# Eleven products of constants and a mark by GpSimd ahead of layer 0's experts

## The chip, the core and the metric

The kernel runs on one core of one Trainium2 chip, in one launch. The metric is the device time of an execution in microseconds. The time before is the median of four runs, 1123.99 us (1120.69 to 1127.42).

## The reference

Two transformer layers on a batch of 8 sequences of 512 tokens with 128 channels, all in float32. Each layer has a recurrent attention (a scan over the 512 steps) and a mixture of experts. The change stands between two parts of layer 0's mixture: the routing, which decides for each token which two of eight experts it goes to and which slot it has there, and the experts themselves. Cut to that:

```python
logits = relu(x @ rw1 + rb1) @ rw2 + rb2
vals, ids = top_k(logits, 2)
probs = softmax(vals)
pos = cumsum(one_hot(ids, 8)) - 1              # the slot in the expert
disp[ids, pos] += x                            # 512 slots for each of 8 experts
h = relu(einsum('enc,ech->enh', disp, ew1) + eb1)
eo = einsum('enh,ehc->enc', h, ew2) + eb2
y = eo[ids, pos] * probs * (pos < 512)         # then summed over the two choices
x = x + y
```

Layer 1 takes the sum `x` as its input.

## The kernel before

The program is a sequence of stages, each with tiles of its own in SBUF and PSUM. Within the two big stages (layer 0's attention with its routing; layer 1) a planner in Python, `Order`, decides the order of the instructions from estimated costs when the program is built. It also puts "fills" (L952) into gaps that it expects on TensorE: products of the identity with a tile of zeros, 128x128 by 128x512, into a PSUM bank that nobody reads. The order is then fixed: every engine works through its own instructions in that order, and waits at semaphores for the others.

**The end of the routing.** `route(b)` handles one sequence of 512 tokens, in four tiles of 128. Its last products on TensorE are the two that count the assignments before each token (L860, L861). VectorE computes from them a slot number for each assignment (L865 to L871), and GpSimd scatters the tokens' rows, 130 numbers each (128 channels, the weight, the place to return to), with eight indirect DMAs of 128 rows (L876) into `row0`, a table in DRAM with 512 slots for each of 8 experts.

**The experts of layer 0** (L1021 on) have an order written out by hand. SyncE issues eight loads (L1023), one for each expert's 512 slots, into tiles `de0[e]`; they wait for the scatters' data. For an expert `e`:

- `prepare0(e)`: four transposes on TensorE (L436, called from L984) into `tr_bank`, and a copy by VectorE into `dT0` (L985).
- `first_half(e)`: four products 128x128 by 128x512 (L990), each into a bank of its own, `mid_banks0[0..3]`, and each followed by ScalarE's relu (L993) into `hT0`.
- `second_half(e)`: four products that add up in `yT_bank` (L997), and ScalarE's bias (L1000).
- `results0(e)`: four transposes back (L1005), VectorE's multiply with the weights (L1006), and four indirect DMAs by GpSimd (L1012), which scatter the results to their tokens in `res0`.

TensorE's order is `prepare0(0)`, then for each expert `first_half(e)`, `results0(e - 1)`, `prepare0(e + 1)`, `second_half(e)`. Expert 0's first instruction on TensorE is so the transpose of its first 128 slots. The experts' weights were loaded earlier, during the scans. In layer 1, `attend(b)` loads the results (`ys`, L1149) and adds them to the tokens on TensorE (L1161).

`ident` (the identity), `zeros` (128x512) and the pool `const` are made at the start of the program and stay. The PSUM pool of the experts takes the banks that the stage before gave back: one for `tr_bank`, four `mid_banks0`, one `yT_bank`, two `y_banks`. A product in float32 stands in the trace as two records, a transpose as one.

Of the kernel before, what the change touches and what calls it, by code (L numbers as in the profile page):

```python
# [9 lines left out]
F32 = mybir.dt.float32  # L10
# [7 lines left out]
P = 128  # L18
# [11 lines left out]
NC0 = H0 // P  # L30
# [159 lines left out]
def two_layers(ctx: ExitStack, tc: tile.TileContext, a: dict, out: bass.AP):  # L190
    nc = tc.nc

    const = ctx.enter_context(tc.tile_pool(name="const", bufs=1))
# [10 lines left out]
    def ring_of(pool, n, shape, name, dtype=F32):  # L204
        return [pool.tile(shape, dtype, tag=f"{name}{i}", bufs=1, name=f"{name}{i}") for i in range(n)]
# [19 lines left out]
    ident = const.tile([P, P], F32, name="ident")  # L225
# [102 lines left out]
    zeros = const.tile([P, S], F32, name="zeros")  # L328
# [650 lines left out]
    mid_banks0 = ring_of(psum, 4, columns, "mid0")  # L979
# [3 lines left out]
    def prepare0(e):  # L983
        transpose_to(tr_bank, de0[e][:, :, 0:C])  # L984
        nc.vector.tensor_copy(dT0[e % 2], tr_bank)  # L985

    def first_half(e):
        for c in range(NC0):
            ps = mid_banks0[c]
            nc.tensor.matmul(  # L990
                ps, lhsT=ew1_all[:, e, c * P : (c + 1) * P], rhs=dT0[e % 2], start=True, stop=True
            )
            nc.scalar.activation(hT0[e % 2][:, c, :], ps, AF.Relu, bias=col(EB1 + e * NC0 + c))  # L993

    def second_half(e):
        for c in range(NC0):
            nc.tensor.matmul(  # L997
                yT_bank, lhsT=ew2_all[:, e, c, :], rhs=hT0[e % 2][:, c, :], start=c == 0, stop=c == NC0 - 1
            )
        nc.scalar.activation(yT0[e % 2], yT_bank, AF.Identity, bias=col(EB2 + e))  # L1000

    def results0(e):
        ps, y = y_banks[e % 2], y0[e % 3]
        for t in range(NT):
            nc.tensor.transpose(chunk(ps, t), chunk(yT0[e % 2], t), ident)  # L1005
        nc.vector.tensor_mul(  # L1006
            y,
            tiled(ps),
            de0[e][:, :, WEIGHT : WEIGHT + 1].to_broadcast(tokens),
        )  # L1010
        for t in range(NT):
            nc.gpsimd.indirect_dma_start(  # L1012
                out=res0_w[e * NT + t],
                out_offset=bass.IndirectOffsetOnAxis(ap=de0[e][:, t, DEST : DEST + 1].bitcast(I32), axis=0),
                in_=y[:, t, :],
                in_offset=None,
                bounds_check=NA0 - 1,
                oob_is_err=False,
            )

    with tc.manual_schedule():  # L1021
        for e in range(E0):
            nc.sync.dma_start(de0[e], row0[e * CAP : (e + 1) * CAP, :].rearrange("(t p) c -> p t c", p=P))  # L1023
        prepare0(0)
        for e in range(E0):
            first_half(e)
            if e > 0:
                results0(e - 1)
            if e + 1 < E0:
                prepare0(e + 1)  # L1030
            second_half(e)
        results0(E0 - 1)
        nc.scalar.preload_act_table_set(EXP)
# [777 lines left out]
```

## Time and profile before

| What | Value |
| --- | --- |
| median of four runs | 1123.99 us (1120.69 to 1127.42) |
| the profiled execution | 1118.28 us |
| its span, first to last instruction | 1116.5 us |
| its mean granted TensorE clock | 0.818 |
| PE busy | 832.2 us (75% of the span) |
| VectorE, ScalarE, GpSimd busy | 625.9, 472.5, 453.1 us |
| fills, L952 | 76 records, 42.9 us busy, mean 694 ns |
| L990 PE | 64 records, 31.6 us busy, mean 641 ns, shortest 592, longest 1219 |
| L1012 GpSimd | 32 scatters, 31.3 us busy, mean 979 ns |

The busy time of an engine is an average over stages that have different limits, so the page's shares don't tell what a few microseconds between two stages are worth. For that the timeline of the stretch is read, and for TensorE also the granted clock: 1.00 is full speed, and 0.50 half of it, at which the same product takes twice as long. A stretch's row gives the clock and how much of it the engine had work. Times are from the span's start; routing ends and the experts start between 360 and 400 us.

### The profile page before, as it was taken

What the parts mean: (1) busy time and instruction counts of PE and PEld (TensorE: products, weight loads), DVE (VectorE), ACT (ScalarE), POOL (GpSimd) and SP (SyncE); (2) the same over time, 40 slices, a digit from 0 to 9 for tenths busy, and PEclk for the clock granted to TensorE, in tenths of its full rate; (3) what the DMA queues carried; (4) which work ended last, traced back from release to release, by engine and by line L of the source; (5) the groups of instructions that cost most, each with busy time, mean ns of one, the idle gap of its engine ahead of it and who ended that gap; (6) DMA issues with size and microseconds to landing.
All of it is one profiled execution on the core that took longest, in us unless ns stands there. A gap on an engine that the chain in (4) does not pass through costs nothing. (4 is left out here: it accounts for less than half of the span.)

```text
span 1116.5 us, 13427 instructions
## 1 busy us (share of the span) xinstructions
PE 832.2 (75%) x3819; PEld 552.8 (50%) x3819; DVE 625.9 (56%) x1592; ACT 472.5 (42%) x1040; POOL 453.1 (41%) x466
## 2 busy tenths in 40 slices
PE   5979898897889399687889598655628677777830
PEld 3545464563546144234656345443318577766730
DVE  5588987698693111266776285452435445554417
ACT  6544655462524044385466554433413233332310
POOL 6200005307445334200053548565553656556550
PEclk9887889779788599898899677777758888899775
DMA  7985666474244300389550175461113222222119
GB/s 180 235 220 130 140 160 189 105 176 100 65 96 145 78 11 15 108 219 221 130 147 20 48 191 159 105 184 39 39 57 102 80 78 82 81 77 81 46 31 358
DMA packets 75531, 131.93 MB, mean 118 GB/s; under 512 B 13044, under 2 KB 54902, under 8 KB 67264
## 3 DMA queue, kind: packets, MB, share of 16 engines
q1 hardware_dynamic: 46400, 91.12, 31.7%
q0 software_dynamic: 14832, 27.84, 8.6%
q10 hardware_dynamic: 14224, 12.11, 3.6%
q8 instruction: 30, 0.49, 0.2%
q14 instruction: 45, 0.37, 0.1%
HBM read 94.79 MB, written 41.14 MB: 122 GB/s over the span
## 5 line engine op out<-in xcount | busy, mean ns | idle before, releaser
L1532 POOL DMA_INDIRECT rows<-rows,si x128 | 152.3, 1190 | 215.6 <-DVE tmp L1502 131.7
L1739 POOL DMA_INDIRECT res<-qy,to x144 | 143.0, 993 | 110.3 <-DVE qw L1701 69.1
L876 POOL DMA_INDIRECT row<-rows,si x64 | 90.0, 1406 | 220.0 <-DVE qT L587 112.2
L1718 ACT ACTIVATE qh<-mid,qw 128x128 f32<-128x128 f32 x288 | 78.7, 383 | 180.3 <-remote 91.6
L1712 PE MATMUL mid<-dT,qw 128*128 128x128 f32 x576 | 88.9, 310 | 42.7 <-issue 35.9
L1712 PEld LDWEIGHTS mid<-dT,qw 128*128 128x128 f32 x576 | 80.6, 219 | 49.9 <-issue 42.0
L1729 PE MATMUL qyp<-qw,qh 128*128 128x128 f32 x576 | 81.6, 302 | 5.9 <-ACT qh L1718 3.9
L671 PE MATMUL acc<-add,center 128*128 128x512 f32 x128 | 75.8, 747 | 10.2 <-DVE add L700 8.4
L1729 PEld LDWEIGHTS qyp<-qw,qh 128*128 128x128 f32 x576 | 78.9, 219 | 5.2 <-ACT qh L1718 4.1
L694 DVE TENSOR_TENSOR_SCAN add<-dec,add 128x2048 f32<-128x2048 f32 x16 | 70.8, 4425 | 0.7
L1737 DVE TENSOR_TENSOR qy<-qyp,de 128x512 f32<-128x512 f32 x36 | 24.8, 688 | 75.1 <-remote 26.4
L1701 DVE COPY qw<-fw 128x258 f32 x144 | 44.0, 306 | 35.3 <-issue 16.8
L179 ACT ACT_TABLE_LOAD x48 | 61.6, 1283 | 5.2 <-issue 3.2
L671 PEld LDWEIGHTS acc<-add,center 128*128 128x128 f32 x128 | 29.9, 244 | 52.8 <-issue 34.0
L1012 POOL DMA_INDIRECT res<-y,de x32 | 31.3, 979 | 46.7 <-DVE dT L985 22.1
L952 PE MATMUL idle_bank<-zeros,ident 128*128 128x512 f32 x76 | 42.9, 694 | 0.8 <-DVE y L1006 0.8
L1702 DVE COPY qw<-fw 128x256 f32 x144 | 42.2, 293 | 2.1 <-issue 1.6
L1317 PE MATMUL acc<-ident,kb 128*128 128x128 f32 x256 | 37.2, 315 | 7.3 <-DVE kb L1307 7.3
L1317 PEld LDWEIGHTS acc<-ident,kb 128*128 128x128 f32 x256 | 36.0, 229 | 11.5 <-DVE kb L1307 11.4
L1696 PE MATMUL qT<-ident,de 128*128 128x128 f32 x144 | 25.5, 289 | 21.8 <-DMA de<-rows 14.1
L789 PE MATMUL bank<-xT,rw 128*128 128x512 f32 x64 | 37.8, 723 | 4.2 <-ACT xT L781 3.8
L662 ACT ACTIVATE dec<-dec 128x2048 f32<-128x2048 f32 x16 | 30.5, 1907 | 21.9 <-DVE dec L682 21.9
(336 smaller groups left out, 1766.6 us busy)
## 6 DMA issues: line engine op xcount, KB each, us to landing
add<-keys SPq DMA_DIRECT2D x16, 1024.0 KB
qb_first<-queries SPq DMA_DIRECT2D x8, 1024.0 KB
qb_second<-queries SPq DMA_DIRECT2D x8, 1024.0 KB
kb<-pairs SPq DMA_DIRECT2D x8, 1024.0 KB
gb_both<-decays SPq DMA_DIRECT2D x8, 1024.0 KB
qb_both<-pairs SPq DMA_DIRECT2D x8, 1024.0 KB
yk<-res SPq DMA_DIRECT2D x8, 1024.0 KB
de<-rows SPq DMA_DIRECT2D x108, 65.0 KB
```

What stands on the lines that cost most here:

```text
L179: self.load(table)
L671: nc.tensor.matmul(acc, lhsT=center, rhs=st[:, j, :], start=g + j == 0, stop=(g + 1) * J + j == D + J - 1)
L694: nc.vector.tensor_tensor_scan(flat, dec.rearrange("p j t -> p (j t)"), flat, 0.0, ALU.mult, ALU.add)
L876: nc.gpsimd.indirect_dma_start(out=row0_w[(b * NT + t) * 2 + k], out_offset=bass.IndirectOffsetOnAxis(ap=m.si[:, t, k : k + 1], axis=0), i ...
L952: nc.tensor.matmul(idle_bank, lhsT=ident, rhs=zeros, start=True, stop=True)
L1317: nc.tensor.matmul(chunk(acc, t), lhsT=chunk(st[:, j, :], t), rhs=ident, start=j + t == 0, stop=j + t == DK + NT - 2)
L1532: nc.gpsimd.indirect_dma_start(out=rows1_w[(b * NT + t) * K1 + k], out_offset=bass.IndirectOffsetOnAxis(ap=m.si[:, t, k : k + 1], axis=0), ...
L1701: nc.vector.tensor_copy(w1_q[:, i, :], fw1[:, bass.ds(at, WE)])
L1712: nc.tensor.matmul(mid[c][:, here], lhsT=w1_q[:, i, c * P : (c + 1) * P], rhs=dT[:, here], start=True, stop=True)
L1718: nc.scalar.activation(hT[:, c, here], mid[c][:, here], AF.Gelu, bias=w1_q[:, i, I1 + c : I1 + c + 1])
L1729: nc.tensor.matmul(ps[:, here], lhsT=hT[:, c, here], rhs=w2_q[:, i, c * C : (c + 1) * C], start=c == 0, stop=c == NC1 - 1,)
L1739: nc.gpsimd.indirect_dma_start(out=res1_w[4 * q + i], out_offset=bass.IndirectOffsetOnAxis(ap=to[:, i : i + 1], axis=0), in_=y[:, i, :], i ...
```

## The change

Ahead of the loads of the slots in the text (and so ahead of expert 0's transposes on TensorE) there are now eight products of the identity with `zeros`, into the bank of `mid_banks0[3]`; then GpSimd sets a new tile `gate0` of one column to zero; a product with `gate0` as its moving operand, into the first column of the same bank, makes TensorE wait for that memset; three more products of the identity with `zeros` follow. On GpSimd the memset stands behind the routing's last scatters. The first real product into `mid_banks0[3]`, expert 0's fourth, starts the bank anew, so nothing of what the eleven write is read.

```diff
+    def warm0(n):
+
+        for _ in range(n):
+            nc.tensor.matmul(mid_banks0[NC0 - 1], lhsT=ident, rhs=zeros, start=True, stop=True)
+
+    gate0 = const.tile([P, 1], F32, name="gate0")
     with tc.manual_schedule():
+        warm0(8)
+        nc.gpsimd.memset(gate0, 0.0)
+        nc.tensor.matmul(mid_banks0[NC0 - 1][:, 0:1], lhsT=ident, rhs=gate0, start=True, stop=True)
+        warm0(3)
         for e in range(E0):
             nc.sync.dma_start(de0[e], row0[e * CAP : (e + 1) * CAP, :].rearrange("(t p) c -> p t c", p=P))
         prepare0(0)
```

## The prediction

> **What bounds the kernel now.** I read the page first (span 1116.5 us), then the order of time on TensorE, GpSimd and SyncE between layer 0's routing and its experts, then the stretches' granted clock. In the timeline of TensorE (start, duration, engine, line, what; in brackets the idle time before it and what ended it):
>
> ```profile
> 363.13 0.63 PE L860 MATMUL bank<-both,before 128*128 128x32 f32 x2 [1.07 <-DVE hot L823]
> 363.82 0.63 PE L861 MATMUL bank<-prior,ones 128*128 128x32 f32 x2
> 382.12 1.09 PE L436 MATMUL tr<-ident,de 128*128 128x128 f32 x4 [17.67 <-DMA de<-row]
> 384.05 6.46 PE L990 MATMUL mid<-dT,ew_all 128*128 128x512 f32 x8 [0.84 <-DVE dT L985]
> 390.34 0.60 PE L436 MATMUL tr<-ident,de 128*128 128x128 f32 x4
> 390.77 3.60 PE L997 MATMUL yTp<-hT,ew_all 128*128 128x512 f32 x8
> 394.21 3.60 PE L990 MATMUL mid<-dT,ew_all 128*128 128x512 f32 x8
> 397.64 0.60 PE L1005 MATMUL yp<-ident,yT 128*128 128x128 f32 x4
> ```
>
> TensorE has nothing for 17.67 us, until expert 0's slots land. Then the same work is slow for expert 0 and fast for expert 1: transposes 1.09 against 0.60, four products (eight records, two to a product) 384.05 to 390.34 = 6.29 against 394.21 to 397.64 = 3.43. The timelines of GpSimd and SyncE show what sets the landing: the last two scatters, then the loads.
>
> ```profile
> 375.39 0.97 POOL L876 DMA_INDIRECT row<-rows,si  x1 [0.30 <-issue]
> 376.67 0.97 POOL L876 DMA_INDIRECT row<-rows,si  x1 [0.30 <-issue]
> 379.12 4.71 SPq L1023 DMA_DIRECT2D de<-row  x8
> ```
>
> Stretches (time, length, busy time and count of PE, PEld, DVE, ACT, POOL; granted clock; DMA share; GB/s) give the reason, expert 0's cold clock:
>
> ```profile
> 358.90:362.32 3.42, 3.16 (x9) 1.58 (x8) 1.51 (x13) 0.00 (x0) 2.78 (x3) 0.50 0.02 2
> 365.73:382.80 17.07, 0.68 (x4) 0.71 (x4) 0.56 (x3) 0.00 (x0) 7.83 (x8) 0.50 0.17 43
> 382.80:386.21 3.41, 2.57 (x5) 1.14 (x5) 0.69 (x1) 0.00 (x0) 0.00 (x0) 0.50 1.14 307
> 386.21:389.62 3.41, 3.41 (x5) 1.34 (x5) 0.00 (x0) 1.43 (x3) 0.00 (x0) 0.50 0.46 111
> 389.62:393.04 3.42, 3.42 (x12) 1.69 (x12) 0.69 (x1) 1.32 (x2) 0.00 (x0) 1.00 0.00 0
> ```
>
> The clock changes only at instants a multiple of 3.41 us apart. A cold stretch busy for 2.57 of 3.41 did not raise it; a full one did, at 389.62. Do products of zeros count as work? Yes: the stretch 519.33 to 522.74 below is cold and four fifths fill products (L952, zeros), and 1.00 follows. How little loses a warm clock? 314.53 to 317.94, with 1.39 busy (41%, the end of a run of fills): the product at 318.62 is cold. A stretch 54% busy (447.65 to 451.06) kept it.
>
> ```profile
> 314.53:317.94 3.41, 1.39 (x5) 0.45 (x3) 3.08 (x21) 0.65 (x2) 2.80 (x3) 1.00 0.99 220
> 318.62 2.06 PE L952 MATMUL idle_bank<-zeros,ident 128*128 128x512 f32 x2
> 519.33:522.74 3.41, 3.41 (x5) 1.25 (x5) 1.13 (x4) 2.83 (x6) 0.00 (x0) 0.50 1.04 235
> 522.74:526.16 3.42, 2.53 (x9) 1.18 (x8) 3.42 (x1) 3.40 (x6) 0.00 (x0) 1.00 0.99 223
> ```
>
> From 390.34 on TensorE has no gap until the last expert, 7.75 us an expert (L997 at 390.77 and 398.52). Its end releases the last results' multiply, their scatters, the loads `ys` and layer 1's first products (at 460.67, after 5.76 us of waiting for `ys`). So what expert 0 gains or loses arrives whole at layer 1.
>
> **The change part by part.** Nothing is removed or moved; 12 products, one memset and one wait (TensorE on GpSimd) are added.
>
> The eight. Cold, records of a fill follow each other by 0.85 us (520.88, 521.73), so a product is 1.71; warm by 0.43, so 0.86. They write a bank of the stage before; if it is that of the counts, they wait for DVE L866, whose read ends at 364.78. Bounds: 364.45 (the end of L861) and 365.1; I take 364.8. The stretch 365.73 to 369.14 is then full, so the clock rises at 369.14: cold until there 4.34 us = 2.54 products, the other 5.46 x 0.86 = 4.70, end 373.84. All this hides in the 17.67 us of idle time; without that cover it would be 9 us.
>
> From 373.84 TensorE waits for the mark. The stretch 372.56 to 375.97 is busy for 1.28 of 3.41 (38%), less than the 41% that lost the clock: I let it fall at 375.97. This is the step that could go either way.
>
> The mark. The last scatter is over at 377.64. A memset of 128x1 on GpSimd lasted 0.10 (at 0.33, the start of the program), and an iota behind a scatter began at once (364.85 after 364.84). So it is done at 377.74 at best; 0.30 more as between scatters; or, as the iota L1527 that followed four scatters of layer 0's results did (start 457.66, 1.99 us idle, ended by a DMA), 1.99 later. I take 378.1 for TensorE's start, between the first two, since a constant's memset has no data to wait for. The one-column product: two records of up to 0.27 (L724, 128x1), 0.5 with its weights. Behind the memset on GpSimd's queue stands nothing until the result scatters at 399.72; SyncE's loads wait for the scatters' data and not for it. On TensorE everything stands behind it: three products, then expert 0.
>
> The three start at 378.6. Cold: two end at 382.02; the stretch 379.38 to 382.80 is full, so the clock rises at 382.80; by then 0.78/1.71 = 46% of the third is done and the rest takes 0.54 x 0.86 = 0.47: end 383.27. The slots had come at 382.12, so the three are **1.15 us in the way**.
>
> Expert 0 then runs warm. To its first product: 1.93 (384.05 - 382.12) less 0.49 (1.09 - 0.60) = 1.44, so 384.71; the products 3.43: 388.14 against 390.34. Expert 1's transposes need its slots then: all eight loads are done by 388 (the DMA share falls to 0 there). Sum: -1.15 late, +0.49 and +2.86 (6.29 - 3.43) of warm clock = **2.2 us gained**, 1114.3 for the span 1116.5 and 1116.1 for its execution's 1118.28.
>
> The instants at which the clock may change need not fall so elsewhere. Moved through 3.41 us: the kernel before reaches 390.34 at the latest some 0.2 later and, with the rise at 387.5 instead of 389.62, 1.06 earlier (half of 2.12). The changed one lies between 387.4 (the three raise the clock early and are out of the way by 382.7) and 388.9 (all three cold, end 383.73). Over both the gain is 0.5 to 2.7, about 1.8 in the middle. With the mark 1.99 late it is 1.4 in this run's position and about nothing on average.
>
> The Trainium skill, TensorE: Matmul & The Clock Gate, Part 1, in its table of the two states, takes the clock back only after a window that is idle. By that rule 372.56 to 375.97, in which the eight end, does not count as idle, and the clock would outlive the mark's wait; the three would end at about 381.2 and the gain be 3.4. The row at 314.53 speaks against it (41% busy and lost), and I go by the row.
>
> **The rivals.** (1) The warmth lasts over the wait. For: 54% busy was enough once. Against: 41% was not. Then the three take 2.57 from 378.6, end 381.2 before the slots, and the whole cold loss goes: 0.49 + 2.86 = 3.35, so 1120.6.
>
> (2) Slower: the three, in TensorE's one order, hold expert 0 back. Place: the end of the third against 382.12. Each microsecond past that costs one, and expert 0's warmth returns at most 3.35; so it decides at a third that ends after 385.5, that is, three cold products from a mark after about 379.8. For: L1527's start 1.99 late would put the mark at 379.83. If the mark comes only with the landing of slots (382.1), the products start at 382.6, end cold at 387.7, and expert 1's transposes come at 387.7 + 1.44 + 3.43 = 392.6: 2.3 lost, 1126.3. Against: the iota at 364.85 started at once.
>
> (3) The change does not do what it says: the products of zeros don't raise the clock, and expert 0 is cold as before behind three cold products that end at 383.73: 1.6 lost, 1125.6. Against: 519.33, and with it 795.81 to 799.22.
>
> **How the numbers follow.** The likeliest is the 2.2 of this run's position; on the median of the runs shown, 1123.99 (0.5% above the profiled execution), about 1122. Chances: forecast 0.60, rival 1 0.15, rival 2 0.13, rival 3 0.12. Forecast's own range: 0.5 to 2.7 gained, 1121.3 to 1123.5, and with the scatter of the four runs (-3.3, +3.4) 1118 to 1127. The range with the rivals: from 1120.6 less the scatter to 1126.3 plus most of it: 1116.5 to 1128.5. Of this kernel a measurement can tell 0.5% (5.6 us) from no change. No case by itself reaches that; what lies beyond comes from scatter and costs unseen: 0.13 of the forecast's 0.60 and 0.06 of rival 1's 0.15 faster; 0.09 of rival 2, 0.04 of rival 3 and 0.02 of the forecast slower. Faster 0.19, slower 0.15, same 0.66.
>
> **What would show it.** Eight products from about 364.8 with a clock of 1.00 within 5 us; an idle stretch to about 378; the mark's product at 378.1; the three ending between 381.2 and 383.8; expert 0's four products in 3.4 us and L436 of expert 1 between 387.4 and 388.9. Wrong if the mark comes after 379.8, if the clock is 0.50 in expert 0's products, if a gap opens before expert 1 (slots not there), or if layer 1's first wait for `ys` grows by what was gained.

## The result and the profile after

The changed kernel took 1120.64 us (median of 44 runs, 1113.15 to 1134.15), the kernel before 1119.52 in the runs beside it (70 runs, 1111.85 to 1127.42). The ratio is 1.001, 95% interval 0.9995 to 1.0024: no difference. Here and below a ratio leaves out runs over 1.5% above the fastest of their kernel (beside the e runs of the table, one of 1097.32 us so takes 19 of the 35 with it), and a difference of means takes every run. The changed kernel's profile has a span of 1118.0 us. TensorE's timeline between routing and experts, in the columns used before:

```profile
361.65 0.64 PE L860 MATMUL bank<-both,before 128*128 128x32 f32 x2 [1.23 <-DVE hot L823]
364.22 8.97 PE L1024 MATMUL mid<-zeros,ident 128*128 128x512 f32 x16 [1.25 <-DVE pos L866]
373.03 0.28 PE L1030 MATMUL mid<-gate,ident 128*128 128x1 f32 x2
373.17 2.82 PE L1024 MATMUL mid<-zeros,ident 128*128 128x512 f32 x6
380.68 1.09 PE L436 MATMUL tr<-ident,de 128*128 128x128 f32 x4 [4.69 <-DMA de<-row]
382.61 6.59 PE L990 MATMUL mid<-dT,ew_all 128*128 128x512 f32 x8 [0.84 <-DVE dT L985]
389.04 0.60 PE L436 MATMUL tr<-ident,de 128*128 128x128 f32 x4
```

The eight products (16 records) end at 373.03, the mark's product follows at once, with no idle time, and so do the three. All eleven are over at 375.99. Then TensorE is idle for 4.69 us, and expert 0 is as slow as before: four products in 382.61 to 389.04 = 6.43 us (6.29 before). GpSimd's and SyncE's timelines show that the mark did not stand where it was meant to:

```profile
20.05 0.12 POOL L1029 MEMSET gate<- 128x1 f32 x1
375.14 0.97 POOL L876 DMA_INDIRECT row<-rows,si  x1 [0.30 <-issue]
377.59 4.94 SPq L1033 DMA_DIRECT2D de<-row  x8
```

The memset ran at 20.05 us, between the loads of the constants, 355 us before the last scatter. In GpSimd's order of the built program it stands behind the load of the constant `fb2` and ahead of the first fill of `row0`; the order of every other instruction is unchanged (so the built program lists it; the profile shows the memset's own place). The statement in the description of the change that it stands behind the routing's scatters is how the text reads, and not what was built. So the hand-written order did not hold the memset behind the instructions of an earlier block: the layer that builds the program put a memset that waits for no data early. The eight waited 1.25 us behind DVE L866, for their PSUM bank; that this alone kept them in place is likely and not shown.

The granted clock by stretches (the fields as before: five engines' busy time, then clock, DMA share, GB/s) gives the rest:

```profile
364.57:367.98 3.41, 3.41 (x5) 1.34 (x5) 0.45 (x2) 0.00 (x0) 1.52 (x2) 0.50 0.01 0
367.98:371.39 3.41, 3.41 (x9) 1.50 (x9) 0.00 (x0) 0.00 (x0) 2.50 (x4) 1.00 0.02 2
371.39:374.81 3.42, 3.42 (x11) 1.67 (x10) 0.00 (x0) 0.00 (x0) 2.81 (x3) 1.00 0.03 3
374.81:378.22 3.41, 1.18 (x3) 0.19 (x1) 0.00 (x0) 0.00 (x0) 1.00 (x2) 1.00 0.02 3
378.22:381.63 3.41, 0.95 (x4) 0.71 (x4) 0.00 (x0) 0.00 (x0) 0.00 (x0) 0.50 0.88 236
```

The zeros raised the clock after one full stretch, as worked out. The stretch in which the eleven end is 35% busy, and it lost the clock 2.5 us before the slots came. The first `ys` product of layer 1 starts 78.81 us after the slots' landing (78.55 before). Nothing was gained, and of the stage nothing lost: three profiles without any products (before, g1_before and g4_tile_only in the table below) lie between 77.93 and 78.99.

### The profile page after: what moved, and what is told of

Its sections match the earlier page's. It is cut to its first block, busy times and chain, and to the rows that moved or that the text cites. A ratio compares the mean times of both kernels' runs of the same rounds, so it can differ in the third digit from the quotient of the medians.

```text
span 1118.0 us, 13476 instructions
## 1 busy us (share of the span) xinstructions
PE 840.6 (75%) x3843; PEld 554.8 (50%) x3843; DVE 626.4 (56%) x1592; ACT 472.6 (42%) x1040; POOL 453.0 (41%) x467
## 4 chain that ended last, share of the span: by engine, by line
PE 37%; issue 19%; DVE 15%; DMA 11%; ACT 6%; another core or an unknown queue 5%; POOL 4%; DVEq 1%; SPq 1%; POOLq 0%; ACTq 0%
PE mid L1722 7%; PE qyp L1739 5%; PE acc L671 2%; DMA gb_both<-decays 2%; DVE x L1782 2%; PE acc L1327 2%; PE bank L789 2%; DMA row<-rows,si 2%; POOL res L1012 2%; DVE add L694 2%; PE bank L623 1%; DMA queries<-qT 1%; PE qT L1706 1%; POOL row L876 1%
## 5 line engine op out<-in xcount | busy, mean ns | idle before, releaser
L952 PE MATMUL idle_bank<-zeros,ident 128*128 128x512 f32 x76 | 40.6, 661 | 0.8 <-DVE y L1006 0.8
```

## The experiments

Four theories are told apart. A: the early memset is the whole reason; products that bridge the wait bring about 3 us. B: a mark in its place holds expert 0 back by as much as the warm clock returns. C: what expert 0 gains does not arrive at the end. D came up after the e runs: the new tile costs time of its own. "Landing" is the start of expert 0's first transpose; "tile" says that the kernel has `gate0`, and "warm" kernels are those whose products reach nearly to the landing.

| Run | What | Landing to expert 1's transposes, us | Landing to layer 1's `ys` product, us | Ratio to before (95%) | Difference of means, all runs, us (95%) |
| --- | --- | --- | --- | --- | --- |
| before | | 8.22 | 78.55 | | |
| after | 8, early mark, 3; tile | 8.36 | 78.81 | 1.001 (0.9995 to 1.0024) | +1.4 ± 1.5 |
| e1_mark | 8, mark, 3; tile | 5.01 | 75.43 | 1.003 (0.9999 to 1.006) | +2.7 ± 2.8 |
| e2_sixteen | 16 | 5.00 | 75.91 | 0.9984 (0.9953 to 1.0016) | -3.4 ± 3.2 |
| e3_eight | 8 | 7.76 | 78.25 | 0.9989 (0.9954 to 1.0023) | +0.2 ± 3.2 |
| e4_bridge | 11, mark, 4; tile | 5.01 | 75.45 | 1.0048 (1.0004 to 1.0091) | +1.0 ± 3.1 |
| g1_before | the kernel before | 8.45 | 78.99 | 1.0018 (0.9989 to 1.0048) | +1.3 ± 2.7 |
| g2_sixteen | as e2 | 5.01 | 75.60 | 0.9995 (0.9965 to 1.0025) | -2.4 ± 2.5 |
| g3_bridge_empty | 11, mark, 4; no tile | 5.00 | 75.42 | 0.9977 (0.9941 to 1.0012) | -2.9 ± 3.0 |
| g4_tile_only | tile and memset | 7.68 | 77.93 | 1.0009 (0.9974 to 1.0043) | +0.5 ± 3.3 |
| h1_bridge | as e4; tile | 5.01 | 75.66 | 0.9978 (0.9953 to 1.0002) | -3.8 ± 2.2 |
| h2_bridge_empty | as g3 | 5.01 | 75.38 | 0.9964 (0.9941 to 0.9987) | -5.1 ± 2.3 |
| h3_mark | as e1; tile | 6.70 | 77.06 | 1.0007 (0.9981 to 1.0033) | +0.4 ± 1.9 |
| h4_mark_empty | 8, mark, 3; no tile | 5.19 | 75.58 | 0.9969 (0.994 to 0.9997) | -4.3 ± 2.7 |

Runs whose names begin alike share a chip and 35 runs of the kernel before (medians 1114.06, 1108.89 and 1123.69 us), 12 runs of each variant; they are compared only among themselves.

### The mark in its place, and the wait bridged

e1_mark queues the memset behind the last scatter:

```diff
-                nc.gpsimd.indirect_dma_start(
+                scattered[0] = nc.gpsimd.indirect_dma_start(
...
         warm0(8)
-        nc.gpsimd.memset(gate0, 0.0)
+        with tc.issue_after(scattered[0].ins):
+            nc.gpsimd.memset(gate0, 0.0)
```

> The changed kernel with the memset queued on GpSimd behind the routing's last scatter, by an edge that only orders the issue. Measure: from the start of L860 (the counts) to expert 1's transposes (the second L436), 27.21 us before (363.13 to 390.34) and 27.39 with the change (361.65 to 389.04). Theory A (the change's memset stood at 20.1 us, so its mark held nothing and the eleven products ended 4.7 us too early): the mark's product now comes 0.1 to 0.5 us after the last scatter, the three end 0.5 us before to 1.6 us after the slots come, the clock is 1.00 before expert 0's first product ends, the stretch is 24.5 to 26.7 us, and 0.5 to 2.7 us are gained over the kernel before, about 1.8. Theory B (a mark in its place holds expert 0 back as much as warmth returns): stretch 27 us or more, no gain.

GpSimd's and TensorE's timelines of e1_mark (two lines added to the text shift the line numbers):

```profile
380.17 0.98 POOL L877 DMA_INDIRECT row<-rows,si  x1 [0.30 <-issue]
381.14 0.13 POOL L1031 MEMSET gate<- 128x1 f32 x1
```

```profile
381.32 0.38 PE L1032 MATMUL mid<-gate,ident 128*128 128x1 f32 x2 [1.58 <-POOL gate L1031]
381.57 2.82 PE L1025 MATMUL mid<-zeros,ident 128*128 128x512 f32 x6
385.83 0.63 PE L437 MATMUL tr<-ident,de 128*128 128x128 f32 x4 [1.44 <-DMA de<-row]
387.31 3.70 PE L991 MATMUL mid<-dT,ew_all 128*128 128x512 f32 x8 [0.84 <-DVE dT L986]
390.84 0.60 PE L437 MATMUL tr<-ident,de 128*128 128x128 f32 x4
```

Now TensorE waits for the mark, which comes 0.17 us after the last scatter, and expert 0 takes 5.01 us where it took 8.22. Theory A holds for the stage and B falls: the three were done 1.44 us before the slots landed. From L860 to expert 1's transposes it is 22.92 us, below the expected range; 1.1 of that is a shorter way from L860 to the landing (17.91 against 18.99 us), which runs with and without products showed (e3_eight 17.91, g4_tile_only 17.84). So the later runs are read from the landing. The whole time, though, did not follow.

e2_sixteen has no mark, and enough products to reach the slots:

```diff
-    gate0 = const.tile([P, 1], F32, name="gate0")
...
-        warm0(8)
-        nc.gpsimd.memset(gate0, 0.0)
-        nc.tensor.matmul(mid_banks0[NC0 - 1][:, 0:1], lhsT=ident, rhs=gate0, start=True, stop=True)
-        warm0(3)
+        warm0(16)
```

> No mark and no memset: sixteen products of zeros straight behind the counts in place of eight, mark and three. With the change eleven ended at 375.85 and the slots came at 380.68, so five more (0.86 each) end at about 380.2. Theory A (only the idle 4.7 us lost the clock): granted clock 1.00 in all of expert 0, its four products 3.4 us, stretch from L860 to the second L436 27.4 - 3.3 = 24.1 us; 24 to 25 where the clock rises later or the products run past the slots; 2.5 to 3.3 us gained. Theory C (expert 0's start is not on the path that sets the end): the stretch gets shorter by as much, but layer 1's first product on ys does not come earlier, or the time is that of the kernel before.

TensorE's timeline of e2_sixteen:

```profile
367.91 15.40 PE L1024 MATMUL mid<-zeros,ident 128*128 128x512 f32 x32 [0.47 <-DVE pos L866]
384.02 0.63 PE L436 MATMUL tr<-ident,de 128*128 128x128 f32 x4 [0.71 <-DMA de<-row]
385.49 3.70 PE L990 MATMUL mid<-dT,ew_all 128*128 128x512 f32 x8 [0.84 <-DVE dT L985]
389.02 0.60 PE L436 MATMUL tr<-ident,de 128*128 128x128 f32 x4
```

The sixteen leave 0.71 us of idle time, and expert 0's four products take 3.53 us (385.49 to 389.02). From the landing 3.2 us are gained.

e3_eight keeps only the eight (`warm0(8)`, the other four lines left out).

> Only the eight products, without mark, memset and the three. Theory A: they end some 7 us before the slots, the clock is 0.50 again in expert 0, stretch 27.2 to 27.5 us, time that of the kernel before. If the three matter even where they stand now (theory: what they add is a cost of their own), this kernel is faster than the changed one by up to 0.1%.

```profile
378.47:381.88 3.41, 0.85 (x2) 0.02 (x1) 0.00 (x0) 0.00 (x0) 1.95 (x2) 1.00 0.03 5
381.88:385.30 3.42, 0.00 (x0) 0.00 (x0) 0.00 (x0) 0.00 (x0) 0.00 (x0) 0.50 0.57 150
385.30:388.71 3.41, 2.33 (x6) 1.44 (x7) 0.69 (x1) 0.00 (x0) 0.00 (x0) 0.50 1.08 280
```

The stretch in which the eight end is 25% busy, the clock is lost, and expert 0 starts cold: 7.76 us, within the 7.68 to 8.45 of the profiles without products, and the time is as before. Eight alone do nothing, and neither did the eleven of the changed kernel.

e4_bridge is e1_mark with `warm0(11)` ahead of the mark and `warm0(4)` behind it.

> Eleven products, the mark behind the last scatter as in e1_mark, then four. Eleven end at about 375.9 in the changed kernel's times, the last scatter at 376.1, so the mark opens with almost no idle time, and four more end at about 380.0, before the slots at 380.7. Theory A: clock 1.00 from 5 us after the first product on, stretch 24 to 25 us, 2.5 to 3.3 us gained, like e2_sixteen but bound to the scatters and not to a count. Theory B: later than e2_sixteen by the products behind the mark, over 1 us.

The stage did what A expects (5.01 us, the mark opening without idle time at 385.75, 0.58 after the last scatter's end). Yet the mean lay 1 us above the kernel before. Of the three kernels with a warm expert 0, the two that kept the tile `gate0` gained nothing in their whole time, and e2_sixteen, without it, did (-3.4 ± 3.2 us). This is what theory D was made from, so the e runs can't also confirm it.

### Is it the tile?

In the built program `gate0` takes 32 bytes per partition, and 368 other tiles stand 32 bytes higher in SBUF; in kernels without it not one tile has moved (the traces don't hold the tiles' places). Four runs, to tell the tile, the stage and scatter apart. g1_before is the kernel before itself; g2_sixteen is e2_sixteen; g3_bridge_empty is e4_bridge with the mark in a tile that is there anyway; g4_tile_only is the kernel before with the tile alone:

```diff
 # g3_bridge_empty, against e4_bridge
-    gate0 = const.tile([P, 1], F32, name="gate0")
+    gate0 = empty[:, 0, 0:1]
...
 # g4_tile_only, against the kernel before
+    gate0 = const.tile([P, 1], F32, name="gate0")
     with tc.manual_schedule():
+        nc.gpsimd.memset(gate0, 0.0)
```

> The kernel before, unchanged, run as if it were a variant. It says what ratio no change at all gives with as many runs. All theories: 1.000, with an interval of about 0.35% to each side (runs of one kernel on one chip lay 5 us either way, standard deviation, in e1_mark's comparison); slots' landing to expert 1's transposes 7.7 to 8.4 us as in the kernel before (8.22).

> The kernel of e2_sixteen once more, for its time alone: there the stretch from the slots' landing to expert 1's transposes was 5.00 us against 8.22 before, and the ratio 0.998 (0.995 to 1.002). Theory A (3.2 us arrive at the end): 0.997, and with the runs of e2_sixteen taken together 2 to 4 us faster. Theory C (layer 1 gives it back): 1.000 or more in both.

> e4_bridge (eleven products, the mark behind the last scatter, four more), but the mark is set in a column of the tile empty, whose last reader, the fills, is long done, so that no new tile is in SBUF. e4_bridge had the short stretch (5.01 us) but the ratio 1.005 (1.000 to 1.009). Theory A, and e4_bridge's ratio only scatter: 0.997 here. Theory D (the new tile, by the places of other tiles in SBUF, costs 0.4% all over the kernel): 0.997 here, but then also g4_tile_only is at 1.004. Theory C: 1.000 or more.

> The kernel before plus the tile gate0 and its memset, which GpSimd does early as in the changed kernel; no products, no mark. Theory D (the tile itself costs): 1.003 to 1.005. Theory A: 1.000. The stretch from the slots' landing to expert 1's transposes as before, 7.7 to 8.4 us.

The kernel before against itself gave 1.0018, so a ratio of this size is scatter. Both warm kernels without the tile lay 2.4 and 2.9 us below. The tile alone cost 0.5 ± 3.3 us: no verdict. So the same pairs again, with and without the tile, on one chip: h1 as e4, h2 as g3, h3 as e1, and h4 as e1 with the mark in `empty`.

> The kernel of e4_bridge once more, with the new tile gate0, which in the built program moves 368 tiles in SBUF up by 32 bytes. So far the warm kernels without a new tile were 2.4 to 3.4 us faster in the mean of their runs than the kernel before beside them (e2_sixteen, g2_sixteen, g3_bridge_empty), those with it 1.0 and 2.7 us slower (e4_bridge, e1_mark). Theory D (the tile's shift costs about 4 us all over the kernel): mean 3 to 5 us above h2_bridge_empty. Theory A (the mark's and products' effect alone; the rest was scatter): the same mean as h2_bridge_empty within 3.5 us and 2 to 4 us below the kernel before.

> The kernel of g3_bridge_empty once more: products and mark as in h1_bridge, the mark in a column of empty, no tile moved. Theories A and D alike: 2 to 4 us below the kernel before. Stretch from the slots' landing to expert 1's transposes 5.0 us.

> The kernel of e1_mark once more (eight, mark behind the last scatter in gate0, three). Theory D: 0 to 3 us above the kernel before and 3 to 5 us above h4_mark_empty. Theory A: 1 to 4 us below the kernel before, as h4_mark_empty.

> As h3_mark, with the mark in a column of empty and no new tile. Theories A and D alike: 1 to 4 us below the kernel before; the clock may be lost between the eight and the mark, then the stretch from the landing is 5 to 6.5 us. With h1 and h2, the two kernels with gate0 against the two without (24 runs each) tell 2.5 us.

The two kernels with the tile lay 3.0 ± 2.1 us above the two without (24 runs each). Theory D forecast 3 to 5 us for each pair: h3 against h4 gave 4.7 ± 2.8, h1 against h2 1.4 ± 2.8. One part of the first is not the tile: h3_mark's profile shows the clock lost once more, just as expert 0's products start, while in h4's it was up again by then (382.49, its products at 383.75). Stretches of h3_mark:

```profile
383.59:387.00 3.41, 1.15 (x7) 0.44 (x5) 0.69 (x1) 0.00 (x0) 0.00 (x0) 1.00 1.00 270
387.00:390.42 3.42, 3.42 (x4) 1.49 (x5) 0.00 (x0) 0.69 (x1) 0.00 (x0) 0.50 1.19 304
```

The three end at 384.09, the slots land at 385.51, the copy of the transposes takes its 0.84: 34% busy, and the clock falls at 387.00, with expert 0's first product at 386.98 (6.70 us). e1_mark, the same kernel, had its instants elsewhere. The pair without such luck, h1 against h2 (5.01 us both), differs by 1.4 us, within scatter.

Taken together: warm kernels without the tile -3.4 ± 3.2, -3.0 ± 2.0 (24 runs against 47, g1_before among them) and -4.7 ± 1.9 us (24 against 35) in the three comparisons, weighted **-3.8 ± 1.3**. With the tile +1.9 ± 2.5 and -1.7 ± 1.8, weighted -0.4 ± 1.5. All nine warm runs together, with and without the tile, lie 2.4 ± 1.1 us below the kernel before. C falls: what the stage gains, 3.2 us, stands undiminished at layer 1's first `ys` product (75.4 to 75.9 us from the landing in the profiles of 5.0 us, with the tile as without) and shows in the whole time.

D is not shown. For it speak the e runs and the two weighted means, 3.4 us apart; but the pair h1 and h2, the tile alone (+0.5 ± 3.3) and the changed kernel (+1.4 ± 1.5) all fit no cost at all. And e4_bridge and h1_bridge are one kernel and gave +1.0 and -3.8, a difference of 4.8 ± 3.8 that no tile can make. Why the place of tiles should cost time was not found either: between the six profiles with it and the eight without, no group of instructions of one kind differs by more than 1.3 us of busy time in all.

The version to keep is g3/h2, bound to the scatters and without a tile: 0.9964 (0.9941 to 0.9987) in h2, and 5.00 and 5.01 us in both profiles.

## Why the prediction was right, and where it was not

**The time**, 1122.0, and no change to be told: right, but not by the sum. The sum's 2.2 us did not come; the stage from the landing lost 0.14 us. That the time came so near is luck: the forecast gain was smaller than the 5.6 us that the prediction said could be told, and the kernel before itself took 1119.52 in 70 runs, where the sum had started from 1123.99. The lower end of the range does not come out of its sum either: 1120.6 less 3.3 is 1117.3 and not 1116.5.

**The step that failed** is the mark: "The last scatter is over at 377.64 ... I take 378.1 for TensorE's start". The bounds ran from 377.74 to 379.83 and asked only what delays a memset behind the scatters, not whether it stands there. It ran at 20.05, and the product waited for nothing. Rival 3, that the change does not do what it says, was right in kind and wrong in mechanism: the zeros do raise the clock.

**The eight**: 364.8 to 373.84 worked out, 364.22 to 373.03 measured with L860 1.48 us earlier; 9.04 against 8.81 us, with the clock up after the first full stretch. The length and the wait for DVE L866 are right. The start is not: 2.57 us behind that of L860, with 1.67 worked out and 1.97 as the upper bound. L866 ended 2.06 us behind it (1.65 before), and the products followed 0.51 us after that, where 0.02 had been taken.

**The loss of the clock**: 38% busy in the stretch where the products end, argued from a row with 41%. The changed kernel lost it at 35%, so the step held. But the busy share has no sharp limit. Rows of h4_mark_empty:

```profile
372.25:375.66 3.41, 1.64 (x4) 0.38 (x2) 0.00 (x0) 0.00 (x0) 2.53 (x3) 1.00 0.03 3
375.66:379.08 3.42, 1.57 (x5) 0.90 (x6) 0.00 (x0) 0.00 (x0) 1.49 (x3) 1.00 0.02 3
379.08:382.49 3.41, 3.23 (x6) 1.09 (x5) 0.00 (x0) 0.00 (x0) 0.00 (x0) 0.50 0.78 192
573.64:577.05 3.41, 1.41 (x7) 0.52 (x5) 1.58 (x8) 0.00 (x0) 2.52 (x5) 1.00 0.97 247
577.05:580.46 3.41, 1.88 (x10) 1.45 (x11) 2.37 (x2) 1.63 (x3) 3.10 (x2) 1.00 1.02 286
```

48% busy kept it and 46% lost it, but 41% at 573.64 kept it too. And rows of the kernel before:

```profile
355.49:358.90 3.41, 3.41 (x29) 3.10 (x28) 0.00 (x0) 1.22 (x2) 2.50 (x4) 1.00 0.02 2
580.77:584.18 3.41, 2.17 (x6) 1.04 (x7) 3.36 (x5) 2.89 (x9) 3.13 (x3) 1.00 0.50 137
584.18:587.60 3.42, 3.42 (x11) 2.18 (x10) 3.38 (x2) 3.04 (x8) 3.12 (x2) 0.50 0.06 19
```

The stretch at 580.77 is 64% busy and lost the clock. The one at 355.49 shows no gap and lost it as well (0.50 from 358.90, in the prediction's own rows); most of its records are products of eight columns (L802). In all fourteen profiles no stretch under 41% kept the clock, so letting it fall at 38% was right; above that the share alone does not decide. Nor does a full cold stretch always raise it: 222.37 to 225.78 of the kernel before is all busy, and 0.50 follows. What is counted beside the busy time (columns, rows) was not tested.

The rule of the Trainium skill that was weighed (TensorE: Matmul & The Clock Gate, Part 1, the table of two states: back to the low clock after an idle window) does not hold here: 35% and 46% are not idle, and both lost it. Going by the row was right.

**The mark where it belongs, and the three**: tested by e1, h3 and h4. The mark's product came 0.17 us after the last scatter's end (0.46 worked out). The three cost nothing, even in h4, the profile nearest to the sum: they started at 377.75 on a clock still full, lost it at 379.08 in the second of them, and ended at 381.92, 0.18 us before the slots, where a cold start and 1.15 us late were worked out. The landing there was 4.77 us behind the last scatter's end, 4.48 before. So 3.0 us came from the stage (8.22 to 5.19) and not 2.2: "1.15 us in the way" was the term mis-sized. Rival 2 fell with it.

**Expert 0's loss** of 3.35 us: 3.2 measured (8.22 to 5.00), and 2.7 to 3.4 against the three profiles without products (7.68 to 8.45). **That it arrives whole**: 78.55 to 75.4 us from the landing to layer 1, and -3.8 ± 1.3 us in the time of warm kernels without a new tile, -2.4 ± 1.1 in that of all warm ones.

**Not thought of**: that a column of four bytes moves the other tiles; that this costs anything is not shown.

## What to carry to other kernels

Where an instruction is to mark a moment, give it a dependence on what happens at that moment, and look in the built order or in the profile where it stands; a place in the text is not a place in time. A clock kept warm over a wait needs products up to nearly the end of the wait: eleven that end 4.7 us early are worth nothing, sixteen that end 0.7 us early 3.2 us, and with a gap of 1.4 us it is luck (e1_mark kept the clock, h3_mark lost it). Borrowing a column that is there anyway avoids the question of the tile. Measure a 0.3% gain from the stage's own stretch in the trace first, for single runs of one kernel have a standard deviation of 3.4 to 5.5 us.

## What was not expected of the hardware

A stretch of 3.41 us can show as busy from end to end and still lose the full clock: 355.49 to 358.90 of the kernel before did, mostly with products of eight columns, while 41% busy at 573.64 of h4_mark_empty kept it. And the scatter of the runs goes with the clock: among the 35 runs of the kernel before in each of the three comparisons, time and mean granted clock are correlated with -0.67, -0.66 and -0.41. So part of the scatter may be how many stretches happen to fall on the warm side; which of the two causes the other was not tested.
